# A decoder layer with 32 experts: the last small tiles of two experts in one matmul tile

## The chip, the cores and the metric

The kernel runs on one core of one Trainium2 chip. The metric is the device time of one execution in microseconds (us): the median of nine runs. A profiled execution of the same program gives the trace that is read below; its own time stands beside its span in the table.

The engines are named as in the profile: PE (TensorE, the matmuls), PEld (its weight loads), DVE (VectorE), ACT (ScalarE), POOL (GpSimd) and SP (SyncE, which issues most DMAs). DMAs are also issued from ACT's queue and, where rows are picked by an index (gathers and scatters), from POOL.

## The reference, cut to what matters

The layer takes `x` of 32 x 128 tokens of 512 numbers and does three things, each on a layer norm of the running sum: differential self-attention, cross-attention, and a mixture of experts. All is float32. Only the third part is touched by the change:

```python
NUM_EXPERTS, TOP_K, N_GROUPS, N_LIMITED_GROUPS = 32, 6, 4, 2
...
scores = jax.nn.sigmoid(x @ gate_w)              # 4096 tokens x 32 experts
# the two best of four groups of experts are left out, then the six best scores are taken
_, selected_experts = jax.lax.top_k(masked_scores, K)
weights = jnp.take_along_axis(original_scores, selected_experts, axis=-1)
weights = weights / jnp.sum(weights, axis=-1, keepdims=True)
sel_flat = selected_experts.ravel()
xs = jnp.repeat(x, K, axis=0)[jnp.argsort(sel_flat)]
group_sizes = jnp.bincount(sel_flat, length=E).astype(jnp.int32)
g = jax.lax.ragged_dot(xs, w_gate, group_sizes)  # 512 -> 352, weights of each expert
u = jax.lax.ragged_dot(xs, w_up, group_sizes)    # 512 -> 352
d = jax.lax.ragged_dot(jax.nn.silu(g) * u, w_down, group_sizes)   # 352 -> 512
...
expert_out = jnp.sum(out * weights[..., None], axis=1)
shared = jax.nn.silu(x @ sw_gate) * (x @ sw_up) @ sw_down
return (expert_out + shared)
```

There are 4096 x 6 = 24576 pairs of a token and an expert, 768 to an expert on average. How many each expert gets is known only when the scores are computed.

## The kernel before

**Order of the whole.** Self-attention over 32 blocks of 128 tokens; cross-attention, block by block, with the routing of each block beside it (`Routing`); then the shared expert (`Shared`) in eight groups of four blocks, and the 32 experts (`Experts`). Three of the shared groups come before the experts and five after them.

**Routing.** For each pair the kernel writes the token's number and weight into a table in DRAM, in which every expert has a region of its own (`enter`, L1028). When all blocks are in, `tiles` (L1036) cuts each expert's list into tiles of 128 pairs, the last one partly empty: it computes the number of tiles of each expert (`n`, L1086 to 1093), the running sum of them (`end`), and for each place in the order of work which expert's tile it is (`eid`), whether the expert is new for its set of weights (`fresh`) and which row of the table holds its pairs (`rows`). `usual` = 208 places are worked off by straight code; a branch on `used` handles more (L1644).

**Before the first tile.** `fetch` gathers the tables (L1320), `arrange` spreads them on DVE, `turn_tables` transposes them on PE (L1351, L1353), and `places` computes the indices on DVE: `run_of` for the gathers of tokens, `into` for the scatters of results, `weight` for the factors. These calls are placed by hand between the matmuls of the third shared group: `between()` takes the next of the list `todo` at 15 points of the group's code.

**The loop over tiles** (`run`, L1508). The order of PE, DVE, ACT and POOL is the program's order. At step i:

- `gate_up(i)` (L1439): PE multiplies the turned tokens `e_xT` by the gate and the up weights, four matmuls of 128 x 128 on 352 columns each (L1447; a float32 matmul shows as two records). ACT takes the SiLU (L1451), DVE multiplies (L1452), and ACT's queue writes the product to DRAM (L1454).
- `turn_in(i + 2)`: DVE transposes gathered tokens (L1434).
- `turn_out(i - 1)`: DVE transposes the product that came back from DRAM (L1473).
- `down(i - 2)` (L1478): three matmuls on 512 columns (L1483), ACT scales the rows by the weights into `e_y` (L1487; two buffers), POOL adds them into the rows of `sum_d` in DRAM with an accumulating scatter (L1488).
- `part_out(i)`: ACT's queue reads the product back in another layout (`e_gr`, L1463).
- `tokens(i + 5)`: POOL gathers the tokens of a later tile by four indirect DMAs (L1422) into `e_xr` (three buffers).
- `weights_in(i + 4)` and `weights_out(i + 2)`: SP loads weights into one of four sets, only if `fresh` says so (L1396, L1408, L1411). The four sets work on four stretches of the order of tiles in turn.

POOL's order per step is thus one scatter and four gathers. All scatters go to the same tensor `sum_d`.

Of the kernel before, what the change touches and what calls it, by code (L numbers as in the profile page):

```python
# [886 lines left out]
class Routing:  # L887
# [148 lines left out]
    def tiles(self, eid, fresh, rows, used, usual):  # L1036
# [54 lines left out]
        nc.vector.tensor_scalar(n_i, n, float(P - 1), None, ALU.add)  # L1091
        nc.vector.tensor_scalar(n_i, n_i, 7, None, ALU.logical_shift_right)
        nc.vector.tensor_copy(n, n_i)
        end = tile("end", [P, NX])
# [29 lines left out]
        nc.vector.tensor_tensor(fresh, other, first, ALU.max)  # L1124

# [139 lines left out]
class Experts:  # L1265
# [14 lines left out]
    def __init__(  # L1280
        self, cm, ctx, table_ds, h3_d, sum_d, w_gate, w_up, w_down, eid, fresh, rows, n_tiles
    ):
        self.cm, self.h3_d, self.sum_d, self.eid, self.fresh = cm, h3_d, sum_d, eid, fresh
# [22 lines left out]
        self.got, self.spread = {}, {}  # L1306
        self.xr, self.xT, self.gu, self.gr, self.guT = {}, {}, {}, {}, {}
# [49 lines left out]
    def places(self):  # L1357

        nc, cp, T, n_tiles = self.cm.nc, self.cp, self.T, self.n_tiles
        entry = self.entry_ps.rearrange("p o j t -> p o (j t)")[:, :, 0:n_tiles]  # L1360
        self.weight = cp.tile([P, n_tiles], F32, name="e_weight")
        nc.vector.tensor_copy(self.weight, entry[:, 1, :])
# [3 lines left out]
        nc.vector.tensor_copy(row, row_i)  # L1366

        self.run_of = cp.tile([P, self.Q, self.NT * P], I32, name="e_run_of")
        nc.vector.tensor_scalar(
            self.run_of, self.parts_ps.rearrange("p t j x -> p t (j x)"), float(self.Q),  # L1370
            float(-self.Q), ALU.mult, ALU.add,
        )
        nc.vector.tensor_scalar(self.run_of, self.run_of, 0.0, row[:, 1:2], ALU.max, ALU.add)
        none = cp.tile([P, n_tiles], F32, name="e_none")
        nc.vector.tensor_scalar(none, entry[:, 0, :], 0.0, row[:, 0:1], ALU.is_equal, ALU.mult)
        self.into = cp.tile([P, n_tiles], I32, name="e_into")
        nc.vector.scalar_tensor_tensor(self.into, entry[:, 0, :], -1.0, none, ALU.add, ALU.add)

    def weights_in(self, i):

        if i >= self.end:
            return
# [17 lines left out]
    def weights_out(self, i):  # L1400

        if i >= self.end:
            return
# [12 lines left out]
    def tokens(self, i):  # L1416

        if i >= self.end:
            return
# [10 lines left out]
    def turn_in(self, i):  # L1430
        if i >= self.end:
            return
        xT = self.xT[i] = self.p2.tile([P, EC, P], F32, name="e_xT")
        self.cm.nc.vector.transpose(  # L1434
            xT.rearrange("p c (t i) -> p c t i", t=self.Q),
            self.xr.pop(i).rearrange("p t (j c) -> p c t j", c=EC),
        )

    def gate_up(self, i):  # L1439
        if i >= self.end:  # L1440
            return
        nc = self.cm.nc
        pgu = self.cm.banks()
        t, s = self.xT.pop(i), i % SETS
        for half, w in enumerate((self.wg[s], self.wu[s])):
            for c in range(EC):
                nc.tensor.matmul(  # L1447
                    pgu[:, half, 0:M], t[:, c, :], w[:, c, :], start=c == 0, stop=c == EC - 1
                )
# [3 lines left out]
        self.gu[i] = self.dram.tile([self.Q, P, self.RUN], F32, name="e_gu_d")  # L1453
        nc.scalar.dma_start(  # L1454
            out=self.gu[i].rearrange("q s m -> s q m"),
            in_=self.gu_s.rearrange("s (q m) -> s q m", q=self.Q),
        )

    def part_out(self, i):
# [3 lines left out]
        self.cm.nc.scalar.dma_start(  # L1463
            out=gr.rearrange("p t m -> p (t m)"),
            in_=self.gu.pop(i).rearrange("q (i t) m -> (q i) (t m)", t=self.Q),
        )
# [11 lines left out]
    def down(self, i):  # L1478
        nc = self.cm.nc
        py = self.cm.banks()[:, 0, :]  # L1480
        t, s = self.guT.pop(i), i % SETS
        for c, (_, n) in enumerate(M_CHUNKS):
            nc.tensor.matmul(  # L1483
                py, t[:n, c, :], self.wd[s][:n, c, :], start=c == 0, stop=c == len(M_CHUNKS) - 1
            )
        y = self.p2.tile([P, E], F32, name="e_y")
        nc.scalar.mul(y, py, self.weight[:, i : i + 1])  # L1487
        nc.gpsimd.indirect_dma_start(  # L1488
            out=self.sum_d[:, :],
            out_offset=bass.IndirectOffsetOnAxis(ap=self.into[:, i : i + 1], axis=0),  # L1490
            in_=y[:, :],
            in_offset=None,
            bounds_check=self.T + P - 1,
            compute_op=ALU.add,
        )

    def begin(self, first, end):

        self.first, self.end, self.last = first, end, None
        for i in range(first, first + SETS):  # L1500
# [3 lines left out]
    def first_tokens(self):  # L1504
        for i in range(self.first, self.first + 3):
            self.tokens(i)

    def run(self):  # L1508


        first, en = self.first, mybir.EngineType
        with self.cm.tc.manual_schedule(engines={en.PE, en.DVE, en.Activation, en.Pool}):
            for i in range(first, first + 2):
                self.turn_in(i)
                self.tokens(i + 3)
            for i in range(first, self.end + 2):
                self.gate_up(i)
                self.turn_in(i + 2)
                if first < i <= self.end:
                    self.turn_out(i - 1)  # L1520
                self.weights_in(i + SETS)
                if i > first + 1:
                    self.down(i - 2)
                    self.weights_out(i - 2 + SETS)
                if i < self.end:
                    self.part_out(i)
                self.tokens(i + 5)
# [182 lines left out]
```

## Time and profile before

| what | value |
|---|---|
| median of nine runs | 3853.39 us (3848.95 to 3863.86) |
| the profiled execution: its time, its span | 3851.06 us, 3849.3 us |
| PE busy in the span | 3768.9 us (98%) |
| DVE, ACT, POOL busy | 2057.2, 1678.5, 2349.6 us |
| gate and up matmuls of the experts (L1447) | 2 x 1664 records, 1053.8 us |
| down matmuls of the experts (L1483) | 832 + 416 records, 604.2 us |
| gathers of tokens (L1422), mean of one | 832, 1020 ns |
| accumulating scatters (L1488), mean of one | 208, 1615 ns |
| first gate and up of the experts on PE | 2022.2 us |
| first shared group after the experts on PE | 3556.7 us |

The span runs from the first to the last instruction of the program. "Busy" of an engine is the union of its instructions; matmuls are pipelined, so a busy PE is not PE at its peak. In a timeline, the columns are start, length, engine, line, operation, output and inputs, count, and in brackets the idle time of the engine before the instruction and what ended it; "issue" means that the profile shows nothing that it waited for.

### The profile page before, as it was taken

Reading aid. Unit: us, or ns where it says so; the run is one execution under the profiler, and the core shown is the slowest. Engines: PE = TensorE matmul, PEld = TensorE weight load, DVE = VectorE, ACT = ScalarE, POOL = GpSimd, SP = SyncE. Lnnn points to the kernel's source line nnn. Section 1 sums busy time; section 2 is a strip of 40 time slices with the busy share of each in tenths; the row PEclk is TensorE's granted clock in tenths of the full one; section 3 lists DMA queues with packets and bytes.
Section 4 is the critical chain, followed back from the end, with each engine's and each line's share of the span. In section 5 each row is a group of like instructions: output and inputs, shape, how many; then the busy total and the mean of one; then the engine's idle time right before and its main releaser. Section 6 shows DMA issues by size and latency. Waiting matters only on the chain. (4 is left out here: it accounts for less than half of the span.)

```text
span 3849.3 us, 58185 instructions
## 1 busy us (share of the span) xinstructions
PE 3768.9 (98%) x19060; PEld 2014.3 (52%) x19060; DVE 2057.2 (53%) x3202; ACT 1678.5 (44%) x4032; POOL 2349.6 (61%) x2582
## 2 busy tenths in 40 slices
PE   8999999899999999999999999999999999999999
PEld 5666666534444444444445555555555555555444
DVE  5888888777787777877223333333333333333111
ACT  6989989847767776766201111111111111111000
POOL 3555554645777777776337777777777777775000
PEclk9999999899999999999999999999999999999999
DMA  3111110121221111111256777776767777776210
GB/s 112 34 34 37 37 37 26 37 86 50 61 61 50 45 50 50 50 46 34 66 157 160 179 165 174 160 180 150 184 157 167 172 185 158 180 161 154 90 55 33
DMA packets 285987, 387.21 MB, mean 101 GB/s; under 512 B 147888, under 2 KB 179248, under 8 KB 285616
## 3 DMA queue, kind: packets, MB, share of 16 engines
q0 software_dynamic: 62912, 109.85, 16.1%
q1 hardware_dynamic: 81792, 190.98, 15.6%
q10 hardware_dynamic: 140976, 82.60, 7.7%
q8 instruction: 154, 2.52, 0.3%
q14 instruction: 153, 1.25, 0.1%
HBM read 617.52 MB, written 143.07 MB: 198 GB/s over the span
## 5 line engine op out<-in xcount | busy, mean ns | idle before, releaser
L1422 POOL DMA_INDIRECT e_xr<-h_d,e_run_of x832 | 849.1, 1020 | 281.2 <-issue 270.6
L695 DVE TENSOR_REDUCE nm<-ps 128x2 f32<-128x1024 f32 x512 | 610.7, 1215 | 112.4 <-PE ps L691 105.9
L718 ACT ACTIVATE xp<-ps 128x1024 f32<-128x1024 f32 x512 | 505.8, 1021 | 265.3 <-PE ps L691 203.6
L1452 DVE TENSOR_TENSOR e_gu<-e_act,ps 128x352 f32<-128x352 f32 x208 | 108.5, 522 | 938.5 <-ACT e_act L1451 938.5
L1483 PE MATMUL ps<-wd,e_guT 128*128 128x512 f32 (+1 forms) x1248 | 570.0, 593 | 2.6 <-issue 2.6
L714 PE MATMUL ps<-xqn,xk 32*128 32x512 f32 x2048 | 527.4, 620 | 20.5 <-ACT xp L718 19.1
L1447 PE MATMUL ps<-wu,e_xT 128*128 128x352 f32 x1664 | 527.0, 460 | 4.0 <-DMA wu<-in_L_ffn_w_up_dram 4.0
L1447 PE MATMUL ps<-wg,e_xT 128*128 128x352 f32 x1664 | 526.8, 459 | 2.3 <-DMA wg<-in_L_ffn_w_gate_dram 2.3
L691 PE MATMUL ps<-xk,xq 32*128 32x512 f32 x2048 | 525.9, 630 | 0.1
L1451 ACT ACTIVATE e_act<-ps 128x352 f32<-128x352 f32 x208 | 96.3, 463 | 888.5 <-PE ps L1447 815.9
L1447 PEld LDWEIGHTS ps<-wg,e_xT 128*128 128x128 f32 x1664 | 314.8, 189 | 236.2 <-issue 100.9
L1447 PEld LDWEIGHTS ps<-wu,e_xT 128*128 128x128 f32 x1664 | 316.4, 190 | 181.4 <-DMA wu<-in_L_ffn_w_up_dram 7.5
L1488 POOL DMA_INDIRECT sum_d<-e_y,e_into x208 | 335.9, 1615 | 119.1 <-issue 71.0
L279 ACT ACTIVATE s<-s,a_nm 128x128 f32<-128x128 f32 x1024 | 395.6, 395 | 5.0 <-DVE a_nm L265 4.6
L1483 PEld LDWEIGHTS ps<-wd,e_guT 128*128 128x128 f32 (+1 forms) x1248 | 237.9, 191 | 246.1 <-issue 203.3
L1487 ACT ACTIVATE e_y<-ps,e_weight 128x512 f32<-128x512 f32 x208 | 142.9, 687 | 417.2 <-PE ps L1483 407.7
L714 PEld LDWEIGHTS ps<-xqn,xk 32*128 32x128 f32 x2048 | 169.1, 184 | 283.9 <-ACT xp L718 123.1
L1473 DVE STREAM_TRANSPOSE e_guT<-e_gr 96x384 f32<-96x384 f32 (+1 forms) x416 | 230.6, 554 | 55.6 <-DMA e_gr<-e_gu_d 47.7
L228 POOL TENSOR_SCALAR k<-kz,a_keep,a_extra 128x256 f32<-128x256 f32 x128 | 82.7, 656 | 286.0 <-ACT kz L227 286.0
L1028 POOL DMA_INDIRECT table_d<-entry,at x192 | 202.2, 1053 | 63.9 <-issue 52.9
L729 PE MATMUL ps<-xp,v 128*32 128x512 f32 x2048 | 233.0, 595 | 7.9 <-ACT xp L718 7.9
L1434 DVE STREAM_TRANSPOSE e_xT<-e_xr 128x512 f32<-128x512 f32 x208 | 226.2, 1087 | 7.9 <-DMA e_xr<-h_d,e_run_of 7.8
(272 smaller groups left out, 5281.3 us busy)
## 6 DMA issues: line engine op xcount, KB each, us to landing
wg<-in_L_ffn_w_gate_dram SPq DMA_DIRECT2D x208, 704.0 KB
wu<-in_L_ffn_w_up_dram SPq DMA_DIRECT2D x208, 704.0 KB
wd<-in_L_ffn_w_down_dram SPq DMA_DIRECT2D x208, 576.0 KB
e_gu_d<-e_gu ACTq DMA_DIRECT2D x208, 192.0 KB
e_gr<-e_gu_d ACTq DMA_DIRECT2D x208, 192.0 KB
wd<-in_L_ffn_w_down_dram SPq DMA_DIRECT2D x208, 128.0 KB
e_xr<-h_d,e_run_of POOLq DMA_INDIRECT x832
xres<-in_x_dram SPq DMA_DIRECT2D x32, 256.0 KB
```

The costliest lines, as they stand in the source:

```text
L279: nc.scalar.activation(s[:, j, c, side, :], s[:, j, c, side, :], AF.Exp, bias=nm[n][:, side, at : at + 1], accum_out=sm[n][:, to : to + 1],)
L691: self.nc.tensor.matmul(sc[:, i, :], q[rows, ts(c, P)], k[rows, :], start=True, stop=True)
L695: self.nc.vector.tensor_reduce(at[:, self.ROW[side], 2 * pair : 2 * pair + 2], sc, AX.X, ALU.max, negate=True)
L714: self.nc.tensor.matmul(sc[:, i, :], k[rows, ts(c, P)], q[rows, :], start=True, stop=True)
L718: self.nc.scalar.activation(e, sc, AF.Exp)
L729: self.nc.tensor.matmul(po[b, side][ts(j, 32), :], self.v2[b % 2][:, c, 2 * j + side, :], es[j // 2][:, j % 2, :], start=c == 0, stop=c == ...
L1422: self.cm.nc.gpsimd.indirect_dma_start(out=xr[:, t, :], out_offset=None, in_=self.h3_d.rearrange("t (q f) -> (t q) f", q=self.Q), in_offse ...
L1434: self.cm.nc.vector.transpose(xT.rearrange("p c (t i) -> p c t i", t=self.Q), self.xr.pop(i).rearrange("p t (j c) -> p c t j", c=EC),)
L1447: nc.tensor.matmul(pgu[:, half, 0:M], t[:, c, :], w[:, c, :], start=c == 0, stop=c == EC - 1)
L1473: self.cm.nc.vector.transpose(t[rows, 0:n, :].rearrange("p c (t i) -> p c t i", t=self.Q), g[rows, :, 0 : 32 * n].rearrange("p t (j c) -> ...
L1483: nc.tensor.matmul(py, t[:n, c, :], self.wd[s][:n, c, :], start=c == 0, stop=c == len(M_CHUNKS) - 1)
L1488: nc.gpsimd.indirect_dma_start(out=self.sum_d[:, :], out_offset=bass.IndirectOffsetOnAxis(ap=self.into[:, i : i + 1], axis=0), in_=y[:, :] ...
```

## The change

Each expert's list is now cut by halves of 64. An expert whose last tile would hold at most 64 pairs gives this rest to a shared tile: two such experts sit in one tile, one in lanes 0 to 63, the other in lanes 64 to 127. There are `mixed` = 8 shared tiles, for at most 16 experts; `usual` is 192 whole tiles. The shared tiles stand in the order of work at every 25th place (12, 37, and so on).

In `tiles`, the number of whole tiles of an expert; a new `halves` finds, for each shared tile and half, the row of the table (`half`) and the expert (`half_eid`):

```diff
-        nc.vector.tensor_scalar(n_i, n, float(P - 1), None, ALU.add)
-        nc.vector.tensor_scalar(n_i, n_i, 7, None, ALU.logical_shift_right)
+        nc.vector.tensor_scalar(n_i, n, float(P // 2 - 1), None, ALU.add)
+        nc.vector.tensor_scalar(n_i, n_i, 6, None, ALU.logical_shift_right)
+        odd_i = tile("odd_i", [P, NX], I32)
+        nc.vector.tensor_scalar(odd_i, n_i, 1, None, ALU.bitwise_and)
...
+        nc.vector.tensor_tensor(n, n, odd, ALU.add)
+        nc.vector.tensor_scalar(n, n, 0.5, None, ALU.mult)
+        nth = tile("nth", [P, NX])
+        nc.vector.tensor_tensor_scan(nth, self.ones[:, 0:NX], odd, 0.0, ALU.mult, ALU.add)
+        alone = tile("alone", [P, NX])
+        nc.vector.tensor_scalar(alone, nth, float(2 * mixed), None, ALU.is_le)
+        nc.vector.tensor_tensor(odd, odd, alone, ALU.mult)
+        nc.vector.tensor_tensor(n, n, odd, ALU.subtract)
```

The indices of the shared tiles are made by four new steps of the kind that the whole tiles have, on 32 partitions, and put into the list of the third shared group behind the gathers of the first three tiles:

```diff
             experts.first_tokens,
+            experts.fetch_halves,
+            nothing,
+            nothing,
+            experts.arrange_halves,
+            experts.turn_halves,
+            experts.places_of_halves,
         ]
```

`fetch_halves` issues four gathers from POOL, `arrange_halves` one addition and four copies on DVE, `turn_halves` six transposes on PE. `places_of_halves` does on DVE what `places` does, and makes for each shared tile two columns of indices, `into_half`: each sends the lanes of the other half to spare rows behind the tokens.

The matmuls of a shared tile (`gate_up`; `down` has the same pattern): each half has its own weights and its own 64 columns of the array.

```diff
+            for half, w in enumerate((self.xg, self.xu)):
+                for c in range(EC):
+                    for h in range(2):
+                        lanes = ts(h, P // 2)
+                        nc.tensor.matmul(
+                            pgu[lanes, half, 0:M], t[:, c, lanes], w[h][:, c, :],
+                            start=c == 0, stop=c == EC - 1,
+                        )
```

The product of a shared tile is written to DRAM and read back by two DMAs each from ACT's queue, one for each half. In `down`, the whole `e_y` is scattered twice, with one column of `into_half` each time:

```diff
+        m = i - self.n_tiles
+        for into in [self.into[:, i : i + 1]] if m < 0 else [self.into_half[:, h, m : m + 1] for h in range(2)]:
+            nc.gpsimd.indirect_dma_start(
+                out=self.sum_d[:, :],
+                out_offset=bass.IndirectOffsetOnAxis(ap=into, axis=0),
+                in_=y[:, :],
+                in_offset=None,
+                bounds_check=self.T + P - 1,
+                compute_op=ALU.add,
+            )
```

The weights of the shared tiles have buffers of their own (`xg`, `xu`, `xd`, two of each, one tile deep). `mixed_loads(m)` loads them from SP, unconditionally, eight DMAs for a tile, one at each step of the loop, from the step after the `down` of the shared tile before:

```diff
+                each(lambda i: self.weights_in(i + SETS), k)
+                each(self.down, k - 2)
+                each(lambda i: self.weights_out(i + SETS), k - 2)
+                next(loads, None)
+                each(self.part_out, k)
+                each(self.tokens, k + 5)
+                m = seq[k - 2] - self.n_tiles + 1 if 2 <= k < len(seq) + 2 else 0
+                if 0 < m < self.mixed:
+                    loads = self.mixed_loads(m)
```

For the room of these buffers, the pools of cross-attention (`x_p2`) and of the early shared groups (`s_p`) are closed before the loop, and a new `s_p` is opened after it for the last five groups:

```diff
+    x_out.close()
+    e_out = ExitStack()
+    experts.mixed_weights(
+        e_out.enter_context(tc.tile_pool(name="e_x", bufs=1, reuse_waits="tile"))
+    )
     experts.run()
...
+    e_out.close()
+    shared.use(ctx.enter_context(tc.tile_pool(name="s_p", bufs=1, reuse_waits="tile")), s_w)
```

## The prediction

> **What bounds the kernel now.** I read the page's slices first, then the expert stage by itself, because that is all the change touches; the page's chain of waits is no help there, since it is followed back only to 3556 us, where the last shared groups run. One window of the expert stage (columns: length, then busy time and instructions of PE, PE's weight loads, DVE, ACT, POOL; clock, DMA share, GB/s):
>
> ```profile
> 2200.00:3500.00 1300.00, 1293.61 (x3888) 738.14 (x3887) 454.80 (x706) 203.14 (x353) 1004.67 (x882) 1.00 0.73 170
> ```
>
> PE looks like the only limit, at full clock. One tile in PE's timeline (start, length):
>
> ```profile
> 2789.75 2.53 PE L1447 MATMUL ps<-wg,e_xT 128*128 128x352 f32 x8
> 2792.12 2.53 PE L1447 MATMUL ps<-wu,e_xT 128*128 128x352 f32 x8
> 2794.49 2.74 PE L1483 MATMUL ps<-wd,e_guT 128*128 128x512 f32 x6
> 2797.06 2.53 PE L1447 MATMUL ps<-wg,e_xT 128*128 128x352 f32 x8
> ```
>
> 2797.06 - 2789.75 = 7.31 us a tile, 4.74 of it gate and up (16 records, 0.296 each), 2.57 down (6 records, 0.43 each). The same stretch of POOL:
>
> ```profile
> 2792.85 1.62 POOL L1488 DMA_INDIRECT sum_d<-e_y,e_into  x1 [0.30 <-issue]
> 2794.78 1.06 POOL L1422 DMA_INDIRECT e_xr<-h_d,e_run_of  x1 [0.30 <-issue]
> 2796.15 1.00 POOL L1422 DMA_INDIRECT e_xr<-h_d,e_run_of  x1 [0.31 <-issue]
> 2797.45 1.01 POOL L1422 DMA_INDIRECT e_xr<-h_d,e_run_of  x1 [0.30 <-issue]
> 2798.76 1.01 POOL L1422 DMA_INDIRECT e_xr<-h_d,e_run_of  x1 [0.30 <-issue]
> 2800.08 1.61 POOL L1488 DMA_INDIRECT sum_d<-e_y,e_into  x1 [0.30 <-issue]
> ```
>
> Four gathers and one scatter, and between any two only the 0.30 us that every POOL DMA has before it. That is 7.23 us a tile without one real wait. The share "busy" of POOL (1004.67 of 1300) leaves those 0.30 out and hides this. Of the 207 distances between scatters (L1488), 158 lie between 7.20 and 7.25. So POOL gains only 0.08 us a tile on PE, and even that is used up. The distance from the end of `e_y` to its scatter is 0.28 us at the first tile, 2.2 at the 103rd, 4.3 at the 199th. What uses it up is this:
>
> ```profile
> 2501.83 1.01 POOL L1422 DMA_INDIRECT e_xr<-h_d,e_run_of  x1 [0.30 <-issue]
> 2505.26 1.61 POOL L1488 DMA_INDIRECT sum_d<-e_y,e_into  x1 [2.43 <-DMA sum_d<-e_y,e_into]
> ```
>
> Each scatter waits until the scatter before it has landed, as both add into `sum_d`. Landing takes 5.0 us from its start (median), which 7.23 hides; behind weight loads it takes up to 8.7. From scatter 1 (2040.2) to scatter 202 (3521.2) POOL needs 1481.0 us, 201 x 7.23 = 1453.2: 27.8 above, of which I count 26 as such late landings, the rest as waits for PE.
>
> **The change, part by part.** The profiled execution took 3851.06 us (span 3849.3), 2.3 below the median of 3853.39. I work on the span and subtract from the median.
>
> *Tiles.* Whether the branch for more than `usual` tiles is taken follows from the inputs: the reference, run on them, gives 32 experts 673 to 842 pairs; before, 207 tiles are needed of 208. Sixteen experts have a last part of 1 to 64, exactly the number that eight shared tiles hold, so 191 whole tiles remain for 192: not taken, with one tile to spare.
>
> *PE.* 208 tiles become 200 if a shared tile costs what a whole one does. Column tiles 64 wide aren't in the trace; the nearest row is 32 wide:
>
> ```profile
> 1502.38 3.64 PE L729 MATMUL ps<-xp,v 128*32 128x512 f32 x32 [0.25 <-ACT xp L718]
> 1505.95 0.70 PE L714 MATMUL ps<-xqn,xk 32*128 32x512 f32 x2
> ```
>
> 32 records of 512 columns in 3.57 us, 0.11 each against 0.43 in a full array: four run side by side. Bounds for two: wholly side by side (0 extra) or wholly one after another (7.31 extra a shared tile, 58.5 in all). I take the first. The way out of that mode costs 3.57 - 8 x 0.43 = 0.13; with gate/up and down of each shared tile between whole tiles there are 4 switches, 32 x 0.13 = 4.2. From the first `e_y` (2039.3) to the last (3555.1) are 1515.8 us now: 205 pitches of 7.31, then 2.6 and 5.5 at the end without gate and up, and 9.2 of stalls for weights. With 200 tiles: 197 x 7.31 + 8.1 + 9.2 + 4.2 = 1461.6. By PE alone the change saves 54.
>
> *POOL.* Eight tiles fewer, but every shared tile scatters twice (`into_half`), the second straight behind the first. The trace holds that case at its end, where no gathers are left:
>
> ```profile
> 3547.95 1.55 POOL L1488 DMA_INDIRECT sum_d<-e_y,e_into  x1 [5.76 <-ACT e_y L1487]
> 3553.78 1.55 POOL L1488 DMA_INDIRECT sum_d<-e_y,e_into  x1 [4.28 <-issue]
> 3559.55 1.55 POOL L1488 DMA_INDIRECT sum_d<-e_y,e_into  x1 [4.22 <-issue]
> ```
>
> 5.83 and 5.77 us from start to start: landing, then about 0.75 until the next starts. Both `e_y` had ended 3.4 us or more before. So a shared tile costs POOL 5.8 more, 46.4 over eight. Bounds: 1.92 each (no wait, 15.4 in all) and 9.5 (the longest landing, 8.7, plus 0.75; 76 in all). Queued behind the second scatter are the gathers of five tiles on, and behind both the buffer of `e_y` (two).
>
> How far may POOL fall behind? `e_y` of tile k+2 overwrites the buffer of tile k, 2 x 7.31 - 0.69 = 13.9 us after the end of `e_y` k; landing takes 5.0, so a scatter 8.9 late holds nobody. Beyond that ACT stands in `e_y`, then the `e_gr` issue behind it, then DVE and PE.
>
> *Weights.* Each shared tile loads two experts anew: 16 x 2.16 MB = 35 MB, in 64 issues on SP's queue, one a step, long before use, beside 67 MB of conditional loads. SP waits, but for loads wanted four tiles on: 0 on the path by itself. What they may do is make landings late: between scatters with one load of about 0.7 MB the trace shows 0 to 0.9 us, mostly 0. I take 8 us for 64 (0.125 each); bounds 0 and 26 (as much again as all loads now, with half the bytes).
>
> *Start.* `halves` and nine operations in `tiles` put about 25 small DVE operations of 0.16 to 0.23 into a stretch where DVE idles 6 us at a time: 0. But `fetch_halves` stands on POOL behind the 12 gathers that end at 2012.35; four more slots of 1.31 and a landing of 3.4 make 2019.7, `arrange_halves` (0.42 + 4 x 0.22) 2021.0. `turn_halves` stands on PE between the two halves of the 20 matmuls of L1247 that begin at 2012.34, so at 2016.7: PE waits 4.3 and then turns for 1.2. I take 5; bounds 1 (short gathers) and 9 (the `places_of_halves` operations ahead of the first `turn_in` as well).
>
> *The rest.* Two `e_gu_d` and two `e_gr` issues instead of one cost ACT 0.7 us a shared tile; ACT is busy 203 of 1300: 0, and up to 0.7 x 8 = 6 without that cover. Pools that move (`s_p` for the last groups) wait for tiles long read: 0. POOL's lag at the end is covered by 48 us of the next group before `sum_d` is read.
>
> **Sum.** POOL has gathers behind its scatters up to tile 193 of 200: 192 x 7.23 + 26 + 8 + 46.4 = 1468.6 us. The lag may grow from 0.3 to 8.9, so PE follows at 1460.0, then 5 pitches and the end, 44.7: 1504.7. That is more than PE's 1461.6, so **POOL becomes the bound** and only 1515.8 - 1504.7 = 11.1 of the 54 are left; less 5 at the start, 6. 3853.4 - 6 = **3847**.
>
> A rule that bears on the 5.8: the Trainium skill, "DMA: Bandwidth & Descriptors", section "Anatomy of one DMA — SWDGE (gpsimd) path", fits 2.0 us plus bytes / 436e3. For the 256 KB of a scatter that estimates 2.6 us, half of what the trace shows, and by it the second scatter would cost about 3.4 and the kernel some 19 us less. The accumulating scatters of this case are the nearer evidence, and I go by them.
>
> **Rivals.**
> - *POOL keeps up, PE stays the bound.* It needs late landings to vanish in the new pacing and the second scatter not to wait. Against it: the three rows above, and 158 of 207 distances at POOL's own pace. 54 - 5 saved: 3804. 14%.
> - *The extra loads fill the DMA queues* (slower). Place: landings of scatters, with POOL's slack gone. DMA share is 0.73 and gains about 0.07. Price: 26 instead of 8 and a start of 9: 6 - 18 - 4 = -16, 3869. It decides from about 14 us of new late landings on (0.22 a load). For it: steps with two loads cost up to 2.2 now. Against: these come one a step. 27%.
> - *It doesn't do what it says:* column tiles of 64 run one after another. PE needs 1461.6 + 58.5 = 1520.1, 3853 + 4 + 5 = 3863. L729 speaks against it. 4%.
> - The forecast, POOL bound with 6 saved, 55%, spread 3835 to 3859 by its unknowns.
>
> **Chances.** 0.2% is 7.7 us, about what a measurement tells from no change. The forecast splits into 0.29 below 3845.7, 0.25 within and 0.01 above 3861.1; the first rival is all faster; the second 0.24 slower, 0.03 within; the third half and half. Faster 0.43, same 0.30, slower 0.27. The range that leaves out two in ten reaches past 3804 only in part and takes in 3869: 3806 to 3870.
>
> **What would show it.** Right: second scatters starting about 5.8 us behind the first, POOL at 7.23 between shared tiles, the lag of scatters near 9 from the third shared tile on, PE pitches of some 13 us at shared tiles, PE busy well under 99% in the stage. Wrong: pitches of 7.31 throughout (first rival); many scatter waits outside shared tiles (second); 64-column records at 0.3 each without overlap (third). A second scatter that doesn't wait would overturn the forecast.

## The result, and the profile after

The changed kernel is slower: 3881.82 us median of 10 runs (3868.2 to 3886.99) against 3854.53 us of the kernel before beside it; the ratio is 1.0067, with a 95% interval of 1.0059 to 1.0076. Forecast were 3847 and a range of 3806 to 3870. Repeated on two later occasions the ratio was 1.0065 and 1.0072.

The profiled execution took 3880.15 us with a span of 3878.4, which is 29.1 above the span before. Cut at the same marks as in the forecast, this splits as follows:

| stretch | before | after | difference | forecast |
|---|---|---|---|---|
| start to the first `e_y` | 2039.3 | 2048.1 | +8.8 | +5 |
| first to last `e_y` | 1515.8 | 1532.8 | +17.0 | -11.1 |
| last `e_y` to the end | 294.2 | 297.5 | +3.3 | 0 |
| mean granted clock of PE | 0.994 | 0.988 | | not in it |

The branch for more than `usual` tiles was not taken: 192 whole tiles ran. Column tiles do what the change says. PE's timeline at the third shared tile (start, length, engine, line, operation, count):

```profile
2502.16 2.59 PE L1596 MATMUL ps<-xg,e_xT 128*64 128x352 f32 x16
2504.57 2.54 PE L1596 MATMUL ps<-xu,e_xT 128*64 128x352 f32 x16
2507.04 2.85 PE L1652 MATMUL ps<-wd,e_guT 128*128 128x512 f32 x6
2509.72 2.53 PE L1588 MATMUL ps<-wg,e_xT 128*128 128x352 f32 x8
```

The 32 records of 64 columns take 4.88 us (2502.16 to 2507.04) where the 16 of 128 columns take 4.74, so each pair runs side by side. The second scatter waits, as forecast. POOL's timeline at a shared tile:

```profile
2530.44 1.62 POOL L1659 DMA_INDIRECT sum_d<-e_y,e_into_half  x1 [1.40 <-ACT e_act L1601]
2535.65 1.58 POOL L1659 DMA_INDIRECT sum_d<-e_y,e_into_half  x1 [3.59 <-DMA sum_d<-e_y,e_into_half]
2537.53 1.09 POOL L1566 DMA_INDIRECT e_xr<-h_d,e_run_of  x1 [0.30 <-issue]
```

The distances of the eight pairs are 5.0 to 6.5 us, 45.7 in all. But the bound is no longer PE or POOL alone. The window of the expert stage that the forecast began with (length, then busy time and instructions of PE, PE's weight loads, DVE, ACT, POOL; clock, DMA share, GB/s):

```profile
2200.00:3500.00 1300.00, 1252.40 (x3853) 699.03 (x3852) 434.38 (x670) 192.56 (x335) 963.13 (x843) 0.99 0.79 190
```

PE stands for 48 us where it stood for 6, and POOL works less than before as well (963 for 1005), though it has a scatter more to do at every shared tile. What PE waits for stands in the list of its waits in the stage (waiting line, what released it: us in total, times, longest), before:

```profile
PE ps L1447 <- DMA wu<-in_L_ffn_w_up_dram: 4.0, 5, 1.6
PE ps L1447 <- DMA wg<-in_L_ffn_w_gate_dram: 2.3, 3, 1.5
```

and after:

```profile
PE ps L1588 <- DMA wu<-in_L_ffn_w_up_dram: 20.5, 10, 4.7
PE ps L1588 <- DMA wg<-in_L_ffn_w_gate_dram: 19.1, 6, 5.0
```

These are the weights of whole tiles, not of shared ones: 39.6 us for 6.3. They come at one place. If the part above 7.31 of every distance between the starts of two gates is summed by the second one's position behind the last shared tile, 50.0 of 81.9 us lie at positions 13 and 14. With these inputs a new expert begins at 13 (whole tiles 24, 48, 72 and so on), and there the loads of the next shared tile end. The runs below are compared by the distance from one `e_y` to the next, less 7.31: 42.6 of 83.3 us follow positions 9 and 10, as the `e_y` of a tile stands two steps behind its gate and these two distances hold the gates of 12 and 13. SP's queue at such a place (the issues of the shared tile's loads, and of one new expert's gate and up weights):

```profile
2546.47 0.36 SPq L1515 DMA_DIRECT2D xg<-in_L_ffn_w_gate_dram  x1
...
2590.65 0.37 SPq L1515 DMA_DIRECT2D xu<-in_L_ffn_w_up_dram  x1
...
2592.67 0.35 SPq L1542 DMA_DIRECT2D wg<-in_L_ffn_w_gate_dram  x1
...
2599.35 0.34 SPq L1542 DMA_DIRECT2D wu<-in_L_ffn_w_up_dram  x1
...
2609.98 0.34 SPq L1515 DMA_DIRECT2D xd<-in_L_ffn_w_down_dram  x1
```

and PE, which ended the tile before at 2597.97:

```profile
2600.33 4.30 PE L1588 MATMUL ps<-wg,e_xT 128*128 128x352 f32 x8 [2.36 <-DMA wg<-in_L_ffn_w_gate_dram]
2606.65 3.94 PE L1588 MATMUL ps<-wu,e_xT 128*128 128x352 f32 x8 [2.02 <-DMA wu<-in_L_ffn_w_up_dram]
```

Four sets of weights exist, yet gate is issued 5.3 us before PE is free for it, and up after. In the kernel before, SP issued both together for whole tile 48, more than 7 us ahead of its gate on PE:

```profile
2362.43 0.36 SPq L1396 DMA_DIRECT2D wg<-in_L_ffn_w_gate_dram  x1
2363.12 0.36 SPq L1396 DMA_DIRECT2D wu<-in_L_ffn_w_up_dram  x1
2369.65 2.53 PE L1447 MATMUL ps<-wg,e_xT 128*128 128x352 f32 x8
```

Eight loads, one a step of the loop, should span 7 x 7.31 = 51.2 us; they span 63.5 here and 62.0 to 71.6 at the others. PE takes 51.3 us for the same seven steps here, so SP falls some 12 us behind while it issues them. The weights also take longer once they are issued: at the seven places (whole tiles 24 to 168) gate lands 6.9 to 8.0 us after its issue, by the updates of its semaphore, where the median of the new experts before was 5.4.

PE's two lines after the change show one more thing: 8 records take 4.30 and 3.94 us instead of 2.53. Two windows of the same execution:

```profile
2560.00:2597.00 37.00, 37.00 (x113) 21.12 (x112) 12.88 (x20) 5.75 (x10) 29.07 (x27) 1.00 0.85 209
2597.00:2612.00 15.00, 10.62 (x22) 5.25 (x21) 2.92 (x5) 1.15 (x2) 9.76 (x9) 0.77 0.82 224
```

The clock granted to PE falls to 0.77 over these 15 us. The clock's own records know only full and half speed; between the first and the last `e_y` half speed was granted for 0 us before and for 41.2 us after, which is 20.6 us of PE's work. The Trainium skill, "TensorE: Matmul & The Clock Gate", Part 1, says that the clock halves after an idle window of about 3.4 us. The records agree as to the length: away from the ends of a trace they are 3.41 us long or a multiple of it, and their starts lie on one grid. But PE need not stand for a whole window. If the expert stage of all 20 traces is cut along that grid, each of the 149 full-speed windows in which PE stood for more than 2.01 us (59%) was followed by half speed, and none in which it stood for less than 1.71 us (50%). Behind half speed, full speed came back after every window in which PE stood for less than 0.33 us.

At the start the round trip of the first product is slow. ACT's timeline before:

```profile
2028.31 0.38 ACTq L1454 DMA_DIRECT2D e_gu_d<-e_gu  x1
2030.48 0.35 ACTq L1463 DMA_DIRECT2D e_gr<-e_gu_d  x1
```

after, with the load that SP issued just ahead of it:

```profile
2034.76 0.36 SPq L1515 DMA_DIRECT2D xg<-in_L_ffn_w_gate_dram  x1
```

```profile
2034.95 0.38 ACTq L1605 DMA_DIRECT2D e_gu_d<-e_gu  x1
2040.23 0.35 ACTq L1623 DMA_DIRECT2D e_gr<-e_gu_d  x1
```

5.28 us instead of 2.17 until the product can be read back. ACT's small transfer is issued just behind the 0.7 MB; that these delay it is read from the order of the lines and was not tried.

### The profile page after: what moved, and what is told of

It reads as the page before. It is cut to its first block, busy times and chain, and to the rows that moved or that the text cites. A ratio compares the mean times of both kernels' runs of the same rounds, so it can differ in the third digit from the quotient of the medians.

```text
span 3878.4 us, 57956 instructions
## 1 busy us (share of the span) xinstructions
PE 3742.6 (96%) x19066; PEld 1978.1 (51%) x19066; DVE 2047.0 (53%) x3207; ACT 1668.7 (43%) x4016; POOL 2321.1 (60%) x2555
## 5 line engine op out<-in xcount | busy, mean ns | idle before, releaser
L1566 POOL DMA_INDIRECT e_xr<-h_d,e_run_of x800 | 817.1, 1021 | 273.4 <-issue 225.7
L1652 PE MATMUL ps<-wd,e_guT 128*128 128x512 f32 (+1 forms) x1152 | 531.2, 597 | 11.7 <-issue 9.3
L1588 PE MATMUL ps<-wg,e_xT 128*128 128x352 f32 x1536 | 494.9, 465 | 23.9 <-DMA wg<-in_L_ffn_w_gate_dram 19.1
L1588 PE MATMUL ps<-wu,e_xT 128*128 128x352 f32 x1536 | 492.6, 464 | 20.5 <-DMA wu<-in_L_ffn_w_up_dram 20.5
L1588 PEld LDWEIGHTS ps<-wg,e_xT 128*128 128x128 f32 x1536 | 293.4, 192 | 246.3 <-issue 115.1
L1659 POOL DMA_INDIRECT sum_d<-e_y,e_into x192 | 310.0, 1615 | 143.2 <-issue 75.6
L1588 PEld LDWEIGHTS ps<-wu,e_xT 128*128 128x128 f32 x1536 | 294.1, 192 | 188.8 <-DMA wu<-in_L_ffn_w_up_dram 26.9
L1652 PEld LDWEIGHTS ps<-wd,e_guT 128*128 128x128 f32 (+1 forms) x1152 | 220.1, 192 | 244.5 <-issue 207.0
L1639 DVE STREAM_TRANSPOSE e_guT<-e_gr 96x384 f32<-96x384 f32 (+1 forms) x400 | 221.4, 553 | 113.4 <-DMA e_gr<-e_gu_d 93.1
L1576 DVE STREAM_TRANSPOSE e_xT<-e_xr 128x512 f32<-128x512 f32 x200 | 217.8, 1089 | 49.0 <-DMA e_xr<-h_d,e_run_of 48.9
```

Source lines behind the costliest of these rows:

```text
L1566: self.cm.nc.gpsimd.indirect_dma_start(out=xr[:, t, :], out_offset=None, in_=self.h3_d.rearrange("t (q f) -> (t q) f", q=self.Q), in_offse ...
L1576: self.cm.nc.vector.transpose(xT.rearrange("p c (t i) -> p c t i", t=self.Q), self.xr.pop(i).rearrange("p t (j c) -> p c t j", c=EC),)
L1588: nc.tensor.matmul(pgu[:, half, 0:M], t[:, c, :], w[:, c, :], start=c == 0, stop=c == EC - 1)
L1639: self.cm.nc.vector.transpose(t[rows, 0:n, :].rearrange("p c (t i) -> p c t i", t=self.Q), g[rows, :, 0 : 32 * n].rearrange("p t (j c) -> ...
L1652: nc.tensor.matmul(py[lanes], t[:n, c, lanes], wd[:n, c, :], start=c == 0, stop=c == last)
L1659: nc.gpsimd.indirect_dma_start(out=self.sum_d[:, :], out_offset=bass.IndirectOffsetOnAxis(ap=into, axis=0), in_=y[:, :], in_offset=None, b ...
```

## The experiments

Theory W: the loads of shared tiles make the weights of whole tiles late. Rival S: the second scatter is what the kernel loses by, and the loads only make landings a little late. All ratios are to the kernel before, measured beside it on the same chip. That kernel took 3853.7 to 3854.2 us on three chips, 3871 and 3902 on two others, so a ratio from one chip is compared with that from another with care. The decisive four, at the end, stand together on one chip.

**Loads for the first shared tile alone.**

```diff
-                m = seq[k - 2] - self.n_tiles + 1 if 2 <= k < len(seq) + 2 else 0
-                if 0 < m < self.mixed:
-                    loads = self.mixed_loads(m)
```

> The shared tiles' weights are loaded for the first shared tile alone; the other seven use those (their sums are then not the reference's). 56 of the 64 extra loads, 30.6 of 35 MB, are gone; both scatters of a shared tile stay. Theory W (the loads on SP's queue make the weights of whole tiles late): the long pitches 9 and 10 tiles after a shared tile, 42.6 us of stall over the stage, vanish, POOL's second scatters remain as the only new cost: 3882 - 40 = about 3840, stage from first to last e_y near 1495. Rival S (the second scatters are what the kernel loses by; loads only make landings a little late): 8 to 10 us less, 3872, and the pitches stay long somewhere, as POOL still lags by 9 us.

3865.06 us, 0.9986 [0.9973, 0.9999]. Positions 9 and 10 hold 2.7 us in sum, and scatters now lag 7 to 9 us behind `e_y` over long stretches, the picture that the forecast had drawn. By the ratios this is 31 us under the changed kernel, nearer to W's 40 than to S's 8 to 10, but the stage, 1518.1, is not the 1495 that W expected.

**One scatter.** The second half's rows are left out.

```diff
+        for into in [self.into[:, i : i + 1]] if m < 0 else [self.into_half[:, 0, m : m + 1]]:
```

> A shared tile scatters its first half alone (the second half's rows are left out of the sums); all loads stay. Theory W: the 42.6 us at positions 9 and 10 stay, since no scatter makes them; what goes is at most the rest, so 3882 - 15 to - 40, about 3855. Rival S: 8 x 5.8 = 46 us less, 3836, and the long pitches at positions 9 and 10 gone.

3875.76 us, 1.0033 [1.0010, 1.0056]. Positions 9 and 10 keep 40.1 us. S falls: without the wait that it blames, the kernel is still slower than before (by the ratios 13 us were gained, not 46).

**Both.**

> Both of the other two runs' edits: loads for the first shared tile alone, and one scatter for each shared tile (seven tiles' weights and eight half tiles' rows left out). Both theories: PE has nothing new to wait for, stage near 1461.6 to 1475 and 3882 - 60 to - 70, about 3815. How the gain splits tells: by W alone most of it is in the run without reloading, by S most in the run with one scatter; if the two single gains add up to well under this one, the two waits cover each other.

3834.82 us, 0.9918 [0.9897, 0.9940], stage 1486.6. The single gains of the stage against 1532.8 are 14.7 and 8.2, the joint one 46.2; by the ratios, 0.0081 and 0.0034 below 1.0067 against 0.0149 together. By the stage the two waits cover each other: while PE stands for weights, POOL catches up, and while POOL is the bound, late weights cost less. The ratios point the same way, but what the joint gain has above the sum, 0.0034, is no more than their intervals allow.

**Small loads.** All 64 issues stay, from the second shared tile on with 16 KB each.

```diff
+                    if m:
+                        to, src = to[:, 0:1, 0:32], src[:, 0:1, 0:32]
```

> All 64 load issues stay on SP's queue in their places, but those of shared tiles 2 to 8 carry 128 x 128 bytes each instead of some 0.36 to 0.72 MB (the sums of these tiles are not the reference's). If W works by the bytes (the transfer of a load delays the round trips of e_gu and e_gr, whose landings SP waits for), this is as fast as loading once, about 3840. If it works by the issues alone (one more turn of the eight semaphores a step, each waited for in order), it is as slow as the changed kernel, 3882. Rival S: 3872, like loading once.

3870.90 us, 1.0002 [0.9990, 1.0015]: 0.0065 of the 0.0081 that loading once brought, and PE's waits for gate and up weights are 5.7 us in place of 39.6. Mostly the bytes; for the issues about 0.0016 are left, some 6 us, and as the intervals overlap this is not told from nothing.

**The changed kernel again**, as the measure for the next three.

> The changed kernel once more, unedited, as the measure for the other three runs on this chip: 1.0067 times the kernel before, stage from first to last e_y some 1533 us, long pitches 9 and 10 tiles behind each shared one.

3881.39 us, 1.0065 [1.0048, 1.0082]. Its profiled execution has a stage of 1547.6 where the first had 1532.8 and a third, on the last chip, 1526.8: single profiles of this kernel differ by some 20 us, so effects are read from the ratios and only places from the profiles.

**Loads in the order of the program.** SP is added to the engines whose order is fixed in `run`, and the edges that hold its loads in order fall away there.

```diff
-        with self.cm.tc.manual_schedule(engines={en.PE, en.DVE, en.Activation, en.Pool}):
+        with self.cm.tc.manual_schedule(engines={en.PE, en.DVE, en.Activation, en.Pool, en.SP}):
```

> The loads on SP's queue keep the order in which the loop names them (SP joins the engines whose order is fixed); the same loads, bytes and scatters. Theory W by order: in the changed kernel a load for a whole tile stands in SP's queue behind waits for round trips of e_gu and e_gr made only a tile or two before that tile, so that it is issued about 8 us ahead of its use though four sets of weights exist; in program order it is issued 20 us or more ahead, the stalls 9 and 10 tiles on vanish, and the kernel comes to what loading once gave, 0.9986 of the kernel before. Rival, W by bytes: the 0.7 MB a step occupy the DMA engines whatever the order, and the weights land late all the same: 1.004 to 1.007.

3879.47 us, 1.0070 [1.0053, 1.0087], no gain; eight loads still span 61.3 to 70.0 us. But this run tests nothing: the 832 loads of weights stand on SP's queue in the same order as in the changed kernel, with the same waits between them. The changed kernel had the order of the program already, so the order alone does not bring the loads forward; whether another order would is open.

**The second scatter later.** Three gathers stand between any two scatters at a shared tile and the two tiles behind it; `e_y` has three buffers.

```diff
+        for n, into in enumerate(
+            [self.into[:, i : i + 1]] if m < 0 else [self.into_half[:, h, m : m + 1] for h in range(2)]
+        ):
+            self.gathers(3 * n)
...
+                if 2 <= k < len(seq) + 2 and seq[k - 2] >= self.n_tiles:
+                    before |= {k + 1: 2, k + 2: 1}
+                self.gathers(before.get(k, 0))
```

> Of a shared tile's two scatters the second stands three gathers later, and the next two scatters follow after three gathers each, so that none starts sooner than 5.85 us after the one ahead; one more buffer for e_y. By the forecast's price a second scatter then costs POOL 1.92 instead of 5.8, 31 us less over the stage. Theory that the two waits cover each other (loading once saved 15 of the stage, one scatter 8, both 46): alone it brings what leaving the second scatter out brought, 1.003 of the kernel before, the stalls at 9 and 10 staying. Rival S: 31 us, 0.9985.

3866.39 us, 1.0049 [1.0027, 1.0072]. Alone it brings little that can be told from nothing (0.0016 under the changed kernel), as covering predicts; 32.6 us stay at position 10.

**Order, scatter and an earlier start together.**

> Program order on SP, the second scatter three gathers later, and the halves' table gathers, copies and turns ahead of the shared group's end (right behind those of the whole tiles) instead of behind the first tokens. If the three causes are those found, the stage comes near 1480, the start loses 6 us less, and the kernel is at 0.989 of the kernel before (about 3812). If bytes make the weights late, some 1.000.

3875.92 us, 1.0068 [1.0050, 1.0085]. A miss: the order on SP is again that of the changed kernel, and the start came later, not earlier (first `e_y` 2053.0). What is left is the later scatter, 0.0019 worse here than alone, within the intervals.

**Loads moved away** from the steps in which new experts are loaded.

```diff
-                next(loads, None)
+                if k < 12 or (k - 12) % 25 in (5, 6, 7, 8, 15, 16, 17, 18):
+                    next(loads, None)
```

> The same 64 loads of shared tiles, same queue and bytes, but from the second shared tile on they are issued in the steps 5 to 8 and 15 to 18 behind a shared tile instead of 3 to 10. With these inputs whole tiles of a new expert are issued on SP in the steps 2, 9, 12 and 19 (their down weights two steps later). Theory W by collision (a load of 0.7 MB just ahead of a new expert's loads of 2.2 MB, which are issued about 8 us before their use in both kernels, makes these land late): the 43 us at positions 9 and 10 fall to about 10, what stays is the POOL bound of loading once, about 0.9995 of the kernel before. Rival, W by sum (the DMA engines lose the same time wherever the loads stand): the stalls move to other positions, 1.005 to 1.007.

3876.12 us, 1.0063 [1.0051, 1.0075]. The stall at positions 9 and 10 falls to 12.2, and 22 us more appear at 1, 12 and 20. The collision explains the place of the stall, not its size: that the stalls move and the sum stays is what the rival, W by sum, expected.

**Halves early.** `fetch_halves` directly behind `fetch`, copies and turns beside those of the whole tiles.

> Only the start is changed: the gathers of the halves' table rows stand on POOL right behind those of the whole tiles, their copies and turns beside those of the whole tiles, in a free buffer of e_xr. The changed kernel's first e_y comes 8.8 us later than before (2048.1 to 2039.3). If the halves' preparation is the cause, it comes at about 2041 and the kernel is at 1.0065 - 0.0018 = 1.0047 of the kernel before; if the delay has another cause (the whole tiles' own gathers landing late), 1.0065.

3881.69 us, 1.0069 [1.0056, 1.0082], first `e_y` at 2052.3. Moving the halves' preparation did not bring the start forward, and in the changed kernel PE's stall there begins at 2010.09, ahead of the halves' first gather at 2011.09. DVE's timeline in this run:

```profile
2010.41 1.08 DVE L1574 STREAM_TRANSPOSE e_xT<-e_xr 128x512 f32<-128x512 f32 x1 [12.72 <-DMA e_xr<-h_d,e_run_of]
2011.42 0.65 DVE L1270 TENSOR_TENSOR s_gu<-s_act,ps 128x512 f32<-128x512 f32 x1
```

DVE waits in its order for the first gathered tokens, and the product that PE needs for the shared group stands behind that wait.

**Moved loads, later scatter, early halves.**

> Loads moved away, second scatter three gathers later with a third buffer of e_y, halves early. If the three terms are those found and each is covered by nothing else: stage near 1480 (PE's own 1461.6, and some 15 of late landings that POOL can no longer make up, since 25 pitches of 7.23 and one more scatter of 1.92 leave it 0.1 us), start 7 less: 0.990 of the kernel before, about 3815. If the loads cost the same wherever they stand: about 1.001.

3854.22 us, 1.0003 [0.9992, 1.0013]. The best kernel of these runs that leaves nothing out, and equal to the one before: 0.0062 under the changed kernel, where the three parts alone came to 0.0014. It lies near the 1.001 that was expected if the loads cost the same wherever they stand. No kernel that leaves nothing out beat the kernel before.

**Loads in pieces**, a third of the size, over 18 steps instead of 8.

```diff
+                for c in range(to.shape[1] if to.shape[0] > 32 else 1):
+                    n = slice(c, c + 1) if to.shape[0] > 32 else slice(0, 2)
+                    with nullcontext() if self.last is None else self.cm.tc.issue_after(self.last.ins):
+                        self.last = nc.sync.dma_start(out=to[:, n], in_=src[:, n])
+                    yield
...
-                next(loads, None)
+                for _ in range(2 if k < 12 or (k - 12) % 25 % 3 == 2 else 1):
+                    next(loads, None)
```

> The same bytes in three times as many loads (24 a shared tile instead of 8, 0.13 to 0.20 MB each), one or two a step over 18 steps instead of one of 0.13 to 0.72 MB over 8. Theory of the burst (a load of 0.7 MB takes some 4 us of the DMA engines, longer than the 2 to 3 us that the round trip of e_gu has to spare; 0.2 MB takes 1 us): most of the 31 us come back, about 1.000 of the kernel before. Rival, the sum of bytes, or the turns of the semaphores: no gain, 1.005 to 1.009.

1.0153 [1.0135, 1.0172] on the chip where the kernel before took 3902 us. The theory of the burst gets no support. With the later scatter:

> The pieces of the run before and the second scatter three gathers later with a third buffer of e_y. Theory of the burst: the stage comes near 1480, the start stays 9 late: 0.992 of the kernel before. Rival, the sum of bytes: as the run with loads moved away and the later scatter, 1.000 to 1.005.

1.0099 [1.0084, 1.0113], above what either side expected. And what is left when both causes go:

> Loads for the first shared tile alone (the sums of seven shared tiles are not the reference's), and the second scatter three gathers later. If the later scatter is as good as none, this is what one scatter and loads once gave together, 0.992 of the kernel before; if its 1.92 us and landing still hold POOL, some 15 us more, 0.996.

0.9928 [0.9914, 0.9943], what one scatter with loads once gave (0.9918, on another chip). As far as chips compare, the later scatter is as good as none.

**Four on one chip.** The kernel before took 3853.69 us there.

> The changed kernel, unedited, as the measure for the other three on this chip: 1.006 to 1.010 of the kernel before, more the slower the chip moves data.

> Loads for the first shared tile alone, as before (seven shared tiles' sums are not the reference's). If the loads cost 31 us under POOL's cover: 0.008 under the changed kernel on this chip.

> Both causes taken away (loads once, second scatter three gathers later): 0.013 to 0.014 under the changed kernel, so that the scatter's share, once loads are gone, is 0.005 to 0.006 (20 to 23 us of the 30.7 that the second scatters take from POOL).

> The loads in 24 pieces a shared tile. If the number of issues on SP's queue is what makes them dear: 0.006 or more above the changed kernel on this chip. If the slower chip alone made them look dear: the same as the changed kernel within 0.002.

| kernel | us | ratio | interval | stage |
|---|---|---|---|---|
| changed | 3878.97 | 1.0072 | 1.0051 to 1.0092 | 1526.8 |
| loads once | 3850.61 | 0.9993 | 0.9982 to 1.0003 | 1499.0 |
| loads once, scatter later | 3836.13 | 0.9959 | 0.9943 to 0.9974 | 1484.4 |
| loads in pieces | 3898.52 | 1.0116 | 1.0099 to 1.0133 | 1555.7 |

Seven of the eight sets of loads cost 28.4 us, the second scatters 14.5 more once the loads are gone (20 to 23 expected). PE's waits for weights, of the changed kernel there:

```profile
PE ps L1588 <- DMA wg<-in_L_ffn_w_gate_dram: 29.5, 8, 6.6
PE ps L1588 <- DMA wu<-in_L_ffn_w_up_dram: 15.9, 10, 3.0
```

and with loads once:

```profile
PE ps L1588 <- DMA wg<-in_L_ffn_w_gate_dram: 6.5, 6, 1.7
...
PE ps L1588 <- DMA wu<-in_L_ffn_w_up_dram: 4.1, 7, 1.0
```

34.8 us of waiting go with the loads, and the half-speed time of PE between the first and the last `e_y` falls from 37.5 to 10.7 us, which is 13.4 us of its work. The later scatter works as drawn up; POOL's timeline at a shared tile of the third kernel:

```profile
2516.39 1.61 POOL L1662 DMA_INDIRECT sum_d<-e_yy,e_into_half  x1 [0.30 <-issue]
2518.31 1.06 POOL L1566 DMA_INDIRECT e_xr<-h_d,e_run_of  x1 [0.30 <-DVE e_gu L1602]
2519.67 1.01 POOL L1566 DMA_INDIRECT e_xr<-h_d,e_run_of  x1 [0.31 <-issue]
2520.99 1.01 POOL L1566 DMA_INDIRECT e_xr<-h_d,e_run_of  x1 [0.31 <-issue]
2522.30 1.62 POOL L1662 DMA_INDIRECT sum_d<-e_yy,e_into_half  x1 [0.30 <-issue]
```

Between the halves' scatters POOL has gathers to do and waits for nothing but its 0.30; so it is at seven of the eight shared tiles. But POOL's waits for a landed scatter of a whole tile are 32.9 us here and 9.2 with loads once alone, which may be where the rest of the expected 20 to 23 went. Pieces cost 19.5 us more than whole loads, for 128 issues more: 0.15 each, which is between the two expectations (23 us or more, and under 8). A piece also reads shorter runs of memory than a whole load, so the issues alone are not shown to be the cause.

## Why the prediction was wrong

**The step that failed is "Weights".** It said of the 64 extra loads: "SP waits, but for loads wanted four tiles on: 0 on the path by itself", and gave them 8 us through late landings of scatters, with bounds of 0 and 26. Seven of the eight sets cost 28.4 us, above the upper bound, and the part put at 0 was the larger: with these loads 34.8 us of PE's waits for the weights of whole tiles go. Landings were not far off: POOL's waits for a landed scatter of a whole tile are 22.5 us in the stage and 19.2 before, and loading once brings them from 21.3 to 9.2 on the last chip. The two kinds of wait overlap, so they come to more than the cost. Weights are not issued four tiles on: a new expert's gate weights were issued a median of 7.9 us before their use already in the kernel before, about one tile, which its trace would have shown. In the changed kernel gate was issued only 2.2 to 5.5 us before PE was free for it at the seven places of the stall. Each issue on SP waits in order, in the changed kernel mostly for landed round trips of `e_gu` and `e_gr`, which share eight semaphore numbers with SP's loads. SP's longest waits in the stage (us in total, times, longest):

```profile
SPq L1557 <- DMA wd<-in_L_ffn_w_down_dram: 254.6, 72, 8.7
SPq L1542 <- DMA e_gr<-e_gu_d: 169.5, 36, 7.8
SPq L1554 <- DMA e_gr<-e_gu_d: 148.2, 32, 9.0
SPq L1542 <- DMA e_gu_d<-e_gu: 120.4, 33, 9.2
```

Round trips issued up to 4 us behind a load of a shared tile take longer to land (medians of 4.8 and 4.4 us, 3.5 and 3.2 elsewhere, in the changed kernel on the last chip). That SP falls behind and that the loads land later is seen; that it is mostly the bytes follows from the small loads. That the issues add to it is not clear of noise there, and the pieces do not show it cleanly. How much each single wait adds is open, as no run changed the semaphores.

**What was missing altogether is the clock.** The forecast took PE's pitch as fixed at full clock. Once PE stands for some 2 us of a 3.4 us window, the next 3.4 or 6.8 us run at half speed: 20.6 us of work in the stage of the profiled execution. Not all of it is on the path, since POOL is often behind anyway, but it adds about half to the 39.6 us of waits for weights; at 2600 the waits are 4.38 us, and the 16 records behind them take 3.18 us longer than two times 2.53.

**Right, with their sizes.** Column tiles run side by side. The switches of the array's mode cost 0.70 us a shared tile (around its gate and up, and again around its down, the starts around the third shared tile are 0.35 us further apart than a whole tile's), 5.6 in all for 4.2. The second scatter costs POOL 5.7 us, 45.7 in all for 46.4. The allowed lag of 8.9 us is about what scatters reach behind the shared tiles. The PE pitches of some 13 us at shared tiles, another sign of the forecast, do not come: 7.4 to 7.7. Without the loads the forecast's sum is 1504.7 - 8 = 1496.7 us for the stage, and the run with loads once on the last chip measured 1499.0 (1518.1 on the chip where the kernel before took 3871 us). With the 14.5 us that the later scatter then gains, this fits POOL as the bound where the loads do not cover it. Two readings of the trace before were a little high: of the 26 us of late landings the trace names a landing for 15.1 us and nothing for 7.2, and of the 9.2 us of stalls for weights its list of waits has 6.3.

**The skill's rule** weighed against the 5.8 (the Trainium skill, "DMA: Bandwidth & Descriptors", "Anatomy of one DMA — SWDGE (gpsimd) path", an estimate of 2.6 us for 256 KB) does not hold here: the median landing of a scatter is 5.1 us after, and the second one starts 5.0 us behind the first at the earliest. The measurement decides.

**The start** took 8.8 us for the forecast's 5, inside its bounds of 1 and 9 but by other steps. The nine operations in `tiles`, costed at 0, stand ahead of `fresh`, and the first weights were issued 1.5 to 2.8 us later; the first gathered tokens reached DVE 12.4 us after their first gather instead of 8.8. PE then stood 2.84 us for `s_gu`, and the clock halved:

```profile
2014.00:2021.00 7.00, 7.00 (x10) 2.51 (x9) 2.26 (x6) 0.00 (x0) 5.47 (x6) 0.52 0.17 48
```

That is 3.4 us of PE's work lost. The turns themselves cost 0.6. 2.84, 3.4 and 0.6 are about the 6.6 by which the first gate matmul is late; the slow first round trip brings the rest. That moving the halves' gathers did not help fits; the chain from the nine operations to the late tokens is read from the trace and was not tried. The 3.3 us at the end were not tried either; PE's clock was halved there for some 10 us.

**The rivals.** The second one named the right part, the extra loads, and the right sign, but its place was right only in part: landings, where most of it was PE's waits for weights. Its price, 3869, was 13 too low. The first (POOL keeps up) and the third (column tiles one after another) are excluded by the rows above.

## What to carry to other kernels

Before a transfer is costed at nothing because it is wanted late, read from the trace how long ahead of their use the other transfers of its queue are issued now; a queue that issues in order and waits for landed transfers of other engines has the slack of its slowest turn, not of its buffers. Two waits that cover each other hide each other in experiments as well: take both away, and then each, on one chip. Compare the order of a queue in the two traces before an edit of that order is taken for a test. And add 1.7 us to a wait of PE for each half-speed window of 3.4 us behind it.

## Not expected of the hardware

- Standing for 2.01 us of a window of 3.41 us was always enough for half speed in the next window, for less than 1.71 us never, so that a stall's place on the grid counts as well as its length; before, the stage of 1516 us had no half speed, after, 41.2 us.
- The same bytes in three times as many loads were dearer, by 19.5 us for 128 loads, though each was small and they were spread over 18 steps instead of 8.
- A 0.7 MB load issued on SP 0.19 us ahead of a 192 KB transfer of ACT went with 3.1 us more until it could be read back (5.28 for 2.17, one case), although they are in different queues.
- Moving two accumulating scatters apart by three gathers (5.9 us from start to start) removed the second one's wait at seven of eight shared tiles, for 1.92 us of POOL's own time; of some 28 us that this spares POOL (43.5 us between the pairs with loads once, 8 x 1.92 then) the kernel gained 14.5.
